# The last steps of a graph layer on one core: two bases a step later, one block's statistics moved, and a quad's second layer ahead of older sums

## The chip, the cores and the metric

The kernel runs on one NeuronCore of one Trainium2 chip. The metric is the device time of one execution in microseconds (us), as the median of several runs. A profiled execution gives the trace. The engines are called as in the profile: PE is TensorE, DVE is VectorE, ACT is ScalarE, POOL is GpSimd and SP is SyncE. "ACTq" and "SPq" are instructions of a queue that only issue transfers.

## What is computed

12500 nodes with 128 features and 400000 edges sorted by destination. Each edge turns its length into 50 radial functions, sends them through two layers to 128 weights, and multiplies those with the projected features of its source node. The products are summed per destination. Each node's sum goes through two more layers, is added to twice the node's features and normalized over the features.

```python
rbf = jnp.exp(-(distances[:, None] - centers) ** 2 / (2.0 * width * width))
cut = 0.5 * (jnp.cos(jnp.pi * distances / CUTOFF) + 1.0) * (distances <= CUTOFF)
W = (jax.nn.silu(rbf @ fw1 + fb1) @ fw2 + fb2) * cut[:, None]
messages = (h[src] @ pw + pb) * W
agg = jax.ops.segment_sum(messages, dst, num_segments=num_atoms)
h_new = h + (jax.nn.silu(agg @ mw1 + mb1) @ mw2 + mb2)
...
y = x + h_new
out = (y - mean(y)) / sqrt(var(y) + eps)        # over the features
```

## The kernel before

The order of all instructions is written out by hand: an engine runs its instructions in the order in which the program issues them, and waits at the first one whose data aren't there.

**Quads.** Edges that are too long to count are left out first; the others are handled in quads of 512 edges, 4 columns of 128. There are 139 quads, 0 to 138 (`NL = 139`). The main loop over `q` and, behind it, steps written out one by one handle quad after quad. The last seven, 132 to 138, are these written steps (the first is `q = NL - 7`). "Step 134" below is what the program issues for quad 134. One step uses:

- `fetch` (L1088): POOL gathers the source rows, one indirect transfer for each column, three or four for a quad, many quads ahead of their use. Quads 133 and 134 have their first column brought row by row by SP and ACT, long before.
- `basis(o)` (L1140, L1144): ACT makes the radial functions of two quads, `2o` and `2o+1`, with a square and an exponential. The exponential needs a table load (ACT_TABLE_LOAD, on ACT) where another function ran before; so do the silu and the square root of other steps.
- `first(o)` (L1156, PE) and `silu(o)` (L1162, ACT): the first layer of the same two quads. Of the last two bases, 68 serves quads 136 and 137, and 69 serves quad 138.
- `second(q)` (L1171 with L1174, PE): the second layer of one quad, into one of four banks of PSUM. Step q calls it for quad q+2.
- `message(q)` (L1189, for row-by-row columns L1186, DVE): the second layer's output times the gathered rows. It frees the bank. The last quad's message is made in four slices, one for each column.
- `place(q)` (L1201, DVE): the one-hot matrices of the destinations, with the cutoff in them.
- `sum_up(q)` (L1221, PE): message times one-hot matrix, into `sums`.
- `add(q)` (L1255, DVE): `sums` is added to the table `aggT`, at two positions.

**Node blocks.** As soon as the destinations of a block of nodes are complete, its nodes are finished in between: `node_first` (L1267 with L1268 on PE, silu L1270 on ACT into `zs`, both through a bank), `node_second` (L347 with L350, PE, into a bank), `node_stats` (L1305 and L1309, DVE: sum with the features, mean and variance), `deviations` (small DVE operations and a square root on ACT, L1325), `scales` (L1335, L1336), `normalize` (L1356 on ACT, or L1353 on DVE) and a transfer to the output (L193, SP or ACT). Blocks are named by their first tile of 128 nodes: 64, 68, 72 and 76 are the last that the loop handles by a computed table (`begin`), 80 and 84 have four tiles, and 88, 90, 92, 94 and 96 have two. `node_x` (L1285, L1288) adds the features of block 96 on PE, and `node_rest` (L1295) its second layer. `load_x` and `store` bring features in and results out.

**Banks.** `second`, `node_first`, `node_second` and `node_x` each take the bank that has been free longest, so that one of them can wait until an engine has emptied that bank.

`keep_busy(n)` (L1439 before, L1442 in the change) runs n matrix multiplications whose result nobody uses.

## Time and profile before

| | |
|---|---|
| median of 3 runs | 720.64 us (720.64 to 723.32) |
| the profiled execution's own time | 718.53 us |
| its span, first to last instruction | 717.0 us |
| busy over the span: PE, DVE, ACT, POOL | 82%, 78%, 56%, 74% |
| mean granted TensorE clock | 0.918 |

The change reaches only the last tenth of the span. The busy time in that part, in stretches of 5 us (clock as a share of full speed):

| stretch (us) | PE | DVE | ACT | POOL | clock |
|---|---|---|---|---|---|
| 675 to 680 | 2.38 | 3.91 | 4.60 | 3.78 | 1.00 |
| 680 to 685 | 5.00 | 2.53 | 2.25 | 3.78 | 1.00 |
| 685 to 690 | 4.34 | 4.05 | 3.58 | 3.78 | 1.00 |
| 690 to 695 | 3.67 | 3.30 | 3.85 | 3.78 | 1.00 |
| 695 to 700 | 2.61 | 3.84 | 1.79 | 3.78 | 0.90 |
| 700 to 705 | 5.00 | 2.72 | 1.43 | 1.06 | 0.76 |
| 705 to 710 | 3.81 | 3.48 | 4.54 | 0.00 | 1.00 |

A row of a timeline below gives the start in us, the busy time in us, engine, line, operation, output and inputs with shapes and count; in brackets stands how long the engine had been idle before it, and what ended that. A row of the chain of waits gives start, length and what the end of the program waited for in that time.

### The profile page before, as it was taken

How to read it: one execution, taken by the hardware profiler on the slowest of the kernel's cores; microseconds unless marked ns; L12 is line 12 of the kernel's file. 1: busy time of each engine (PE TensorE's matmuls, PEld its weight loads, DVE VectorE, ACT ScalarE, POOL GpSimd, SP SyncE). 2: the span in 40 equal slices, each digit the busy share in tenths (PEclk: the TensorE clock that was granted, in tenths of full speed). 3: DMA queues.
4: the chain of work that ended last, by engine and by line, in shares of the span. 5: the costliest groups of instructions: out<-in, count | busy, mean ns of one | idle time of the engine just before them, and what ended most of it. 6: DMA issues, size and time to landing. Idle time of an engine off the chain costs nothing.

```text
span 717.0 us, 14503 instructions
## 1 busy us (share of the span) xinstructions
PE 584.6 (82%) x3526; PEld 461.1 (64%) x3526; DVE 561.7 (78%) x1741; ACT 401.7 (56%) x569; POOL 529.2 (74%) x565
## 2 busy tenths in 40 slices
PE   5878868688898788697878997799998887878775
PEld 5767557566676576575666765577686654665554
DVE  8899899759998799989979994876856545555765
ACT  6557625245645667554645566466765843574564
POOL 6777777777777777777777777777777777777771
PEclk9998787899999899889987999699999998999997
DMA  8996533333334333443344334444543444344242
GB/s 259 328 328 206 161 99 102 98 102 84 115 103 130 83 87 100 118 126 85 87 113 118 99 116 116 130 131 120 153 113 91 138 111 114 101 142 126 56 131 79
DMA packets 54004, 91.41 MB, mean 127 GB/s; under 512 B 14272, under 2 KB 21536, under 8 KB 53914
## 3 DMA queue, kind: packets, MB, share of 16 engines
q0 software_dynamic: 17712, 36.51, 20.4%
q1 hardware_dynamic: 24916, 35.61, 15.0%
q10 hardware_dynamic: 11286, 18.31, 8.0%
q8 instruction: 29, 0.48, 0.3%
q14 instruction: 61, 0.50, 0.2%
HBM read 74.59 MB, written 15.79 MB: 126 GB/s over the span
## 4 chain that ended last, share of the span: by engine, by line
POOL 18%; DVE 15%; DMA 13%; issue 13%; PE 9%; ACT 3%; ACTq 3%; DVEq 1%; SPq 0%; POOLq 0%
POOL quad L1088 14%; DMA quad<-proj,srci 8%; POOL x L1088 3%; DVE hot L1201 3%; PE ph L1156 3%; DMA x<-proj,srci 3%; DVE msg L1189 2%; ACTq L1064 2%; PE sums L1221 2%; PE bank L1174 1%; DVE aggT L1255 1%; DMA packed<-line,at_i 1%; DVE quad L1189 1%; DMA pair<-packed 1%; DVE quad L1201 1%
## 5 line engine op out<-in xcount | busy, mean ns | idle before, releaser
L1088 POOL DMA_INDIRECT quad<-proj,srci x402 | 381.7, 950 | 122.6 <-issue 97.3
L1174 PEld LDWEIGHTS bank<-fw_sb,s 128*128 128x128 f32 x1112 | 158.1, 205 | 60.3 <-issue 50.2
L1174 PE MATMUL bank<-fw_sb,s 128*128 128x128 f32 x1112 | 158.2, 289 | 0.0
L1156 PE MATMUL ph<-rbf,w_sb 102*128 102x512 f32 x278 | 143.7, 642 | 12.3 <-ACT s L1162 8.3
L1221 PEld LDWEIGHTS sums<-hot,msg 128*128 128x128 f32 x816 | 109.2, 200 | 53.4 <-issue 26.0
L1162 ACT ACTIVATE s<-ph 128x1024 f32<-128x1024 f32 x70 | 71.2, 1017 | 122.3 <-PE ph L1156 121.9
L1201 DVE TENSOR_SCALAR hot<-iota_n,dl,cut 128x80 f32<-128x80 f32 (+4 forms) x408 | 111.1, 347 | 22.9 <-PE sums L1221 20.9
L1221 PE MATMUL sums<-hot,msg 128*128 128x80 f32 (+4 forms) x816 | 111.5, 282 | 15.4 <-DVE msg L1189 15.2
L1088 POOL DMA_INDIRECT x<-proj,srci x94 | 90.0, 958 | 28.7 <-issue 22.3
L1171 PE MATMUL bank<-fb_b,ones_b 96*128 96x512 bf16 x139 | 56.0, 403 | 42.2 <-DVE msg L1189 22.0
L1189 DVE TENSOR_TENSOR msg<-bank,quad 128x512 f32<-128x512 f32 (+1 forms) x78 | 52.5, 673 | 41.1 <-DMA quad<-proj,srci 34.5
L1156 PEld LDWEIGHTS ph<-rbf,w_sb 102*128 102x128 f32 x278 | 51.2, 205 | 51.7 <-issue 37.3
L1255 DVE TENSOR_TENSOR aggT<-aggT,sums 128x80 f32 (+4 forms) x209 | 54.1, 259 | 30.7 <-PE sums L1221 12.4
L1140 ACT ACTIVATE rbf<-d_sb,rbf_bias,rbf_scale 102x512 f32<-102x512 f32 x70 | 56.2, 803 | 8.0 <-issue 8.0
L1088 POOL DMA_INDIRECT quad<-in_x_dram,srci x48 | 47.5, 990 | 15.9 <-issue 12.5
L1162 ACT ACT_TABLE_LOAD x34 | 43.6, 1283 | 15.3 <-issue 14.9
L1144 ACT ACT_TABLE_LOAD x35 | 44.9, 1283 | 11.4 <-issue 9.6
L1221 PE MATMUL sums<-quad,quad 128*128 128x128 f32 (+3 forms) x296 | 41.8, 285 | 11.0 <-DVE quad L1189 11.0
L350 PEld LDWEIGHTS bank<-pw_sb,xT 128*128 128x128 f32 (+1 forms) x292 | 42.3, 209 | 11.2 <-issue 5.6
L1144 ACT ACTIVATE rbf<-rbf 102x512 f32<-102x512 f32 x70 | 44.1, 630 | 7.9 <-issue 5.6
L1221 PEld LDWEIGHTS sums<-quad,quad 128*128 128x128 f32 x296 | 38.6, 201 | 12.7 <-DVE quad L1189 12.4
L350 PE MATMUL bank<-pw_sb,xT 128*128 128x128 f32 (+1 forms) x292 | 42.8, 293 | 0.8 <-ACT xT L995 0.6
(281 smaller groups left out, 796.9 us busy)
## 6 DMA issues: line engine op xcount, KB each, us to landing
d_sb<-near_d ACTq DMA_DIRECT2D x67, 256.0 KB
row_sb<-proj SPq DMA_DIRECT2D x1024, 0.5 KB
x<-in_x_dram SPq DMA_DIRECT2D x46, 256.0 KB
row_sb<-proj ACTq DMA_DIRECT2D x512, 0.5 KB
quad<-proj,srci POOLq DMA_INDIRECT x402
proj<-hp SPq DMA_DIRECT2D x24, 256.0 KB
out_dram<-x SPq DMA_DIRECT2D x22, 256.0 KB
x<-proj,srci POOLq DMA_INDIRECT x94
```

The costliest lines, as they stand in the source:

```text
L350: nc.tensor.matmul(to[:m, k, :], lT[:, k * P:k * P + m], w, start=False, stop=(k == a + c - 1))
L1088: g = nc.gpsimd.indirect_dma_start(out=got[:, j, :], out_offset=None, in_=proj if table is None else table, in_offset=bass.IndirectOffsetO ...
L1140: a = nc.scalar.activation(rbf[:u], d[:u], AF.Square, bias=rbf_bias[:u], scale=rbf_scale[:u])
L1144: nc.scalar.activation(rbf[:u], rbf[:u], AF.Exp, scale=-1.0 / (2.0 * width * width))
L1156: nc.tensor.matmul(ph[:, h, :], w1_sb[:2 * KR, h, :], rbf[:2 * KR], start=True, stop=True)
L1162: nc.scalar.activation(s[:, :n], ph[:, :n], AF.Silu)
L1171: nc.tensor.matmul(pu, ones_b[:, :P], bias_b["fb2"].rearrange("k j f -> k (j f)"), start=True, stop=False)
L1174: nc.tensor.matmul(pu[:, j * H:(j + 1) * H], s[:, j * P:(j + 1) * P], fw2_sb, start=False, stop=(j == QT - 1))
L1189: nc.vector.tensor_mul(msg[:, a:b, :], pu_of[q].rearrange("p (j f) -> p j f", j=QT)[:, a:b, :], got_of[q][:, a:b, :])
L1201: nc.vector.tensor_scalar(hot[:, j, :wide(q)], iota_n[:, :wide(q)], dl[:, at[0], at[1]], cut[:, at[0], at[1]], op0=OP.is_equal, op1=OP.mult)
L1221: nc.tensor.matmul(pa[:, k * W:k * W + wide(q)], msg[:, j, :], hot[:, j, :wide(q)], start=(j % n == 0), stop=(j % n == n - 1))
L1255: nc.vector.tensor_add(to, to, pa[:, k * W:k * W + wide(q)])
```

## The change

No work of the computation is added or left out. Only the order changes, with five more `keep_busy` multiplications and one more pair of table loads.

- **Bases.** The loop no longer calls `basis` for the last two bases in its last step (131). The written step 132 calls them at its end, behind its node work. Their `first` and `silu` follow in steps 133 and 134.
- **Statistics.** The deviations of blocks 64, 68 and 72 are taken without block 76, at the statistics of 72 (step 129). Block 76 joins 80, 84, 88 and 90, whose deviations are taken in step 135. Its own statistics stand at the end of step 130.
- **Second layer.** In each written step, `second(q + 2)` now stands between the message and `sum_up(q)`; before, it stood behind `sum_up(q)`. In the same way `node_second` of 90 and 92, and `node_x`, come ahead of sums, and `first` in steps 133 and 134.
- **The end.** Normalizing of 76 and 80 stands together in step 136, block 88 is normalized on DVE, and `keep_busy` is called with 3, 2 and 2 in place of 1 and 1.

```diff
@@ nodes
-            if begin[t0][2] == q:
+            if begin[t0][2] == q and t0 != early[-1]:
                 if k % 4 == 0:
                     st_of[0] = statistics()
                 node_stats(t0, st_of[0][:, k % 4 * 4:])
-                if k % 4 == 3:
+                if k % 4 == 3 or t0 == early[-2]:
                     deep.append(deviations(early[k // 4 * 4:k + 1], st_of[0]))
@@ tail
+        if q == NL - 9:
+            last_st.append(statistics())
+            node_stats(early[-1], last_st[0])
@@ main loop
-                if 2 * o < NL:
+                if 2 * o < NL and q < NL - 8:
                     basis(o)
@@ written steps
 q = NL - 7
 house(q)
-sum_up(q, message(q))
+msg = message(q)
 second(q + 2)
+sum_up(q, msg)
+node_second(84)
+node_stats(80, last_st[:, 4:])
 bases_of(list(range(q, NL)))
 place(q + 1)
-scales(*deep.pop(0))
+for o in (octs(q), octs(q + 1)):
+    basis(o)
 add(q)
-first(octs(q))
-silu(octs(q))
-node_second(84)
 normal(1)
-st = statistics()
-node_stats(80, st)
 
 q += 1
 house(q)
-sum_up(q, message(q))
+msg = message(q)
 second(q + 2)
-first(octs(q))
-silu(octs(q))
-normal(1)
+first(octs(q - 1))
+silu(octs(q - 1))
+sum_up(q, msg)
 place(q + 1)
+node_stats(84, last_st[:, 8:])
 add(q)
 node_first(88)
...
 q += 1
 house(q)
-sum_up(q, message(q))
+msg = message(q)
 second(q + 2)
+node_x(96)
+sum_up(q, msg)
 place(q + 1)
-node_x(96)
 st = statistics()
+scales(*dev)
 add(q)
 node_first(92)
-scales(*dev)
-normal(1)
+normal(2)
 place(q + 2)
 
 p, q = NL - 2, NL - 1
 house(p)
-sum_up(p, message(p))
+msg = message(p)
 node_second(92)
+keep_busy(3)
+sum_up(p, msg)
+node_stats(92, st)
 sum_up(q, message(q, (0, 1)), (0,))
 add(p)
 node_first(94)
+sum_up(q, message(q, (1, 2)), (1,))
 normal(1)
-sum_up(q, message(q, (1, 2)), (1,))
-node_stats(92, st)
 add(q, (0,))
+keep_busy(2)
 sum_up(q, message(q, (2, 3)), (2,))
-normal(2)
+normalize(*ready.pop(0), on=(0, 1))
+store()
+normal(1)
 node_second(94)
-keep_busy(1)
 sum_up(q, message(q, (3, 4)), (3,))
 add(q, (1,))
 node_first(96)
 node_stats(94, st[:, 2:])
+keep_busy(2)
 dev = variances([92, 94], st)
-keep_busy(1)
```

How it moves instructions at three places. First ACT, from the silu of block 80 on (`zs_10699`, and `zs_10724` in the change) to the silu of basis 68 (`s_10814`, and `s_10853` in the change); `rbf` are the last two bases, and `x41` to `x44` are blocks 64 to 76. Before:

```order
L1270 ACTIVATE zs_10699<-bank3_170 128x512
L1325 ACT_TABLE_LOAD
L1325 ACTIVATE dev_10714<-v_10709,eps_121 128x16
L1140 ACTIVATE rbf_10724<-d_sb,rbf_bias_155,rbf_scale_154 102x512
L1144 ACT_TABLE_LOAD
L1144 ACTIVATE rbf_10724<-rbf_10724 102x512
L1140 ACTIVATE rbf_10728<-d_sb,rbf_bias_155,rbf_scale_154 102x512
L1144 ACTIVATE rbf_10728<-rbf_10728 102x512
L1270 ACT_TABLE_LOAD
L1270 ACTIVATE zs_10755<-bank1_168 128x512
L1162 ACTIVATE s_10814<-ph_10811 128x1024
```

Now:

```order
L1270 ACTIVATE zs_10724<-bank3_170 128x512
L1356 ACTIVATE x42_88<-x42_88,by_10671,rs_10670 128x128 x4
L1270 ACTIVATE zs_10762<-bank2_169 128x512
L1140 ACTIVATE rbf_10822<-d_sb,rbf_bias_155,rbf_scale_154 102x512
L1144 ACT_TABLE_LOAD
L1144 ACTIVATE rbf_10822<-rbf_10822 102x512
L1140 ACTIVATE rbf_10826<-d_sb,rbf_bias_155,rbf_scale_154 102x512
L1144 ACTIVATE rbf_10826<-rbf_10826 102x512
L1356 ACTIVATE x43_89<-x43_89,by_10671,rs_10670 128x128 x4
L1162 ACT_TABLE_LOAD
L1162 ACTIVATE s_10853<-ph_10850 128x1024
```

The silu of block 84 (`zs_10755`, now `zs_10762`) has come from behind the square root, both bases and a table load to ahead of them; block 72 is normalized between the bases and the silu of basis 68.

Second PE, steps 132 and 133. `hot0` is the one-hot matrix of quad 132 and `hot1` that of 133; `ph` is the first layer of basis 68; the two rows L347 and L350 are `node_second(84)`. Before, from the sums of 132 on:

```order
L1221 MATMUL sums_10762<-hot0_1075,msg0_1080 128x128 x4
L1171 LDWEIGHTS ones_b_130
L1171 MATMUL bank1_168<-fb2_b_133,ones_b_130 128x512
L1174 MATMUL bank1_168<-fw2_sb_118,s_10642 128x128 x4
L1156 MATMUL ph_10811<-rbf_10724,w1_sb_114 128x512 x2
L347 LDWEIGHTS ones_b_130
L347 MATMUL bank0_167<-mb2_b_135,ones_b_130 128x512
L350 MATMUL bank0_167<-mw2_sb_120,zs_10755 128x128 x4
L1221 MATMUL sums_10762<-hot1_1192,msg1_680 128x128 x4
```

Now, from the second layer of 134 on:

```order
L1171 MATMUL bank2_169<-fb2_b_133,ones_b_130 128x512
L1174 MATMUL bank2_169<-fw2_sb_118,s_10651 128x128 x4
L1221 MATMUL sums_10774<-hot0_1075,msg0_1080 128x128 x4
L347 LDWEIGHTS ones_b_130
L347 MATMUL bank0_167<-mb2_b_135,ones_b_130 128x512
L350 MATMUL bank0_167<-mw2_sb_120,zs_10762 128x128 x4
L1171 LDWEIGHTS ones_b_130
L1171 MATMUL bank3_170<-fb2_b_133,ones_b_130 128x512
L1174 MATMUL bank3_170<-fw2_sb_118,s_10651 128x128 x4
L1156 MATMUL ph_10850<-rbf_10822,w1_sb_114 128x512 x2
L1221 MATMUL sums_10774<-hot1_1192,msg1_680 128x128 x4
```

The second layer of 134 has moved ahead of the sums of 132, and that of 135 ahead of the sums of 133; the first layer of basis 68 now stands right ahead of the sums of 133, and `node_second(84)` two items earlier.

Third PE in step 136 (`hot0` is quad 136, `hot1` quad 137; L1285 and L1288 are `node_x(96)`, L1267 and L1268 `node_first(92)`). Before:

```order
L1221 MATMUL sums_10971<-hot0_1075,msg0_1080 128x128 x4
L1171 LDWEIGHTS ones_b_130
L1171 MATMUL bank2_169<-fb2_b_133,ones_b_130 128x512
L1174 MATMUL bank2_169<-fw2_sb_118,s_10851 128x128 x4
L1285 LDWEIGHTS ones_b_130
L1285 MATMUL bank0_167<-mb2_b_135,ones_b_130 128x256
L1288 MATMUL bank0_167<-x43_89,ident_68 128x128 x2
L1288 MATMUL bank0_167<-x43_89,ident_68 84x128 x2
L1267 LDWEIGHTS mb1_b_134
L1267 MATMUL bank3_170<-ones_b_130,mb1_b_134 128x256
L1268 MATMUL bank3_170<-aggT_99,mw1_sb_119 128x256
L1221 MATMUL sums_10971<-hot1_1192,msg1_680 128x128 x4
```

Now:

```order
L1171 MATMUL bank3_170<-fb2_b_133,ones_b_130 128x512
L1174 MATMUL bank3_170<-fw2_sb_118,s_10889 128x128 x4
L1285 LDWEIGHTS ones_b_130
L1285 MATMUL bank1_168<-mb2_b_135,ones_b_130 128x256
L1288 MATMUL bank1_168<-x43_89,ident_68 128x128 x2
L1288 MATMUL bank1_168<-x43_89,ident_68 84x128 x2
L1221 MATMUL sums_10976<-hot0_1075,msg0_1080 128x128 x4
L1267 LDWEIGHTS mb1_b_134
L1267 MATMUL bank0_167<-ones_b_130,mb1_b_134 128x256
L1268 MATMUL bank0_167<-aggT_99,mw1_sb_119 128x256
```

The second layer of 138 and `node_x(96)` have moved from behind the sums of 136 to ahead of them.

More of the change, by code (lines that the diff above doesn't have):

```diff
@@ L1425, in nodes @@
                 load_x(t0)
-    st_of, deep = {}, []
+    st_of, deep, last_st = {}, [], []
     def tail(q):
+        if q == NL - 9:
+            last_st.append(statistics())
+            node_stats(early[-1], last_st[0])
         for k, t0, step in ((9, 80, node_first), (8, 80, node_second), (8, 84, node_first)):
@@ L1645, in normal @@
             store()
-    assert not todo and counted and not ready and len(deep) == 1 and done[0] == NL - 7
+    assert not todo and counted and not ready[1:] and not deep and done[0] == NL - 7
+    last_st = last_st[0]
     q = NL - 7
     house(q)
-    sum_up(q, message(q))
+    msg = message(q)
     second(q + 2)
+    sum_up(q, msg)
+    node_second(84)
+    node_stats(80, last_st[:, 4:])
     bases_of(list(range(q, NL)))
     place(q + 1)
-    scales(*deep.pop(0))
+    for o in (octs(q), octs(q + 1)):
+        basis(o)
     add(q)
-    first(octs(q))
-    silu(octs(q))
-    node_second(84)
     normal(1)
-    st = statistics()
-    node_stats(80, st)
     q += 1
     house(q)
-    sum_up(q, message(q))
+    msg = message(q)
     second(q + 2)
-    first(octs(q))
-    silu(octs(q))
-    normal(1)
+    first(octs(q - 1))
+    silu(octs(q - 1))
+    sum_up(q, msg)
     place(q + 1)
+    node_stats(84, last_st[:, 8:])
     add(q)
     node_first(88)
-    node_stats(84, st[:, 4:])
     load_x(92)
@@ L1677 @@
     house(q)
-    sum_up(q, message(q))
+    msg = message(q)
     second(q + 2)
+    first(octs(q - 1))
+    silu(octs(q - 1))
+    sum_up(q, msg)
     node_second(88)
@@ L1682 @@
     add(q)
-    normal(1)
     node_first(90)
-    node_stats(88, st[:, 8:])
+    node_stats(88, last_st[:, 12:])
     load_x(94)
-    normal(1)
     q += 1
     house(q)
-    sum_up(q, message(q))
+    msg = message(q)
     second(q + 2)
     node_second(90)
+    sum_up(q, msg)
     place(q + 1)
+    node_stats(90, last_st[:, 14:])
+    dev = deviations([76, 80, 84, 88, 90], last_st)
+    silu_next()
     add(q)
     load_x(96)
-    node_stats(90, st[:, 10:])
-    dev = deviations([80, 84, 88, 90], st)
-    silu_next()
     q += 1
     house(q)
-    sum_up(q, message(q))
+    msg = message(q)
     second(q + 2)
+    node_x(96)
+    sum_up(q, msg)
     place(q + 1)
-    node_x(96)
     st = statistics()
+    scales(*dev)
     add(q)
     node_first(92)
-    scales(*dev)
-    normal(1)
+    normal(2)
     place(q + 2)
```

## Prediction

> **What bounds the kernel now.** I read the chain of waits first, then POOL's timeline, then DVE's, and asked for each of the last quads how long its message waited, or was late. The chain ends its long stretch of gathers at quad 131:

> ```profile
> 644.16 2.45 DMA quad<-proj,srci
> ...
> 652.90 4.10 DMA quad<-proj,srci
> ...
> 667.90 2.50 DMA quad<-proj,srci
> ```

> A gather lands 2.5 us after its start (4.1 once). POOL starts them 1.25 us apart, with 0.30 us of idle time each, up to the last one. These are the last gathers of quads 131, 134, 135, 136 and 137, and all four of 138:

> ```profile
> 667.90 0.94 POOL L1088 DMA_INDIRECT quad<-proj,srci  x1 [0.30 <-issue]
> ...
> 680.44 0.94 POOL L1088 DMA_INDIRECT quad<-proj,srci  x1 [0.30 <-issue]
> ...
> 685.44 0.94 POOL L1088 DMA_INDIRECT quad<-proj,srci  x1 [0.30 <-issue]
> ...
> 690.43 0.94 POOL L1088 DMA_INDIRECT quad<-proj,srci  x1 [0.30 <-issue]
> ...
> 695.44 0.94 POOL L1088 DMA_INDIRECT quad<-proj,srci  x1 [0.30 <-issue]
> 696.68 0.94 POOL L1088 DMA_INDIRECT quad<-proj,srci  x1 [0.30 <-DVE st L1309]
> 697.93 0.94 POOL L1088 DMA_INDIRECT quad<-proj,srci  x1 [0.30 <-issue]
> 699.18 0.94 POOL L1088 DMA_INDIRECT quad<-proj,srci  x1 [0.30 <-issue]
> 700.42 0.94 POOL L1088 DMA_INDIRECT quad<-proj,srci  x1 [0.30 <-issue]
> ```

> The messages of 131, 134, 135, 136, 137 and the last two slices of 138:

> ```profile
> 670.53 0.69 DVE L1189 TENSOR_TENSOR quad<-bank,quad 128x512 f32<-128x512 f32 x1 [0.85 <-DMA quad<-proj,srci]
> ...
> 686.97 0.55 DVE L1189 TENSOR_TENSOR quad<-bank,quad 128x384 f32<-128x384 f32 x1
> ...
> 692.12 0.69 DVE L1189 TENSOR_TENSOR quad<-bank,quad 128x512 f32<-128x512 f32 x1
> ...
> 697.34 0.69 DVE L1189 TENSOR_TENSOR msg<-bank,quad 128x512 f32<-128x512 f32 x1
> ...
> 701.37 0.68 DVE L1189 TENSOR_TENSOR msg<-bank,quad 128x512 f32<-128x512 f32 x1
> ...
> 706.29 0.48 DVE L1189 TENSOR_TENSOR quad<-bank,quad 128x128 f32<-128x128 f32 x2
> ```

> Start plus 2.5 us against start of the message: quad 131 lands at 670.4 and starts at 670.5. Then 134 is 4.0 us late (682.9 against 687.0), 135 4.2, 136 4.4, 137 3.4, and the last slice of 138, which lands at 702.9 and starts at about 706.5, is 3.6 late. So up to 131 the gathers bound the kernel, and behind it the order of the other engines does. The 3.6 us are what an order can win ahead of the last slice; POOL itself stays, since the change leaves its instructions alone.

> Where the lateness arises is seen on ACT and PE:

> ```profile
> 675.34 1.12 PE L1268 MATMUL bank<-aggT,mw_sb 128*128 128x512 f32 x2 [0.30 <-DVE aggT L1255]
> ...
> 679.72 0.38 PE L1171 MATMUL bank<-fb_b,ones_b 96*128 96x512 bf16 x1 [2.32 <-ACT zs L1270]
> ...
> 683.66 1.06 PE L1221 MATMUL sums<-hot,msg 128*128 128x128 f32 x8
> 684.55 0.38 PE L1171 MATMUL bank<-fb_b,ones_b 96*128 96x512 bf16 x1
> 684.77 1.05 PE L1174 MATMUL bank<-fw_sb,s 128*128 128x128 f32 x8
> 685.66 1.02 PE L1156 MATMUL ph<-rbf,w_sb 102*128 102x512 f32 x2
> 686.52 0.27 PE L1267 MATMUL bank<-ones_b,mb_b 96*128 96x256 bf16 x1
> 686.64 0.59 PE L1268 MATMUL bank<-aggT,mw_sb 128*128 128x256 f32 x2
> 687.11 1.40 PE L1221 MATMUL sums<-quad,quad 128*128 128x128 f32 x8
> ```

> ```profile
> 673.65 0.80 ACT L1140 ACTIVATE rbf<-d_sb,rbf_bias,rbf_scale 102x512 f32<-102x512 f32 x1
> ...
> 677.78 1.28 ACT L1270 ACT_TABLE_LOAD   x1
> 679.07 0.60 ACT L1270 ACTIVATE zs<-bank 128x512 f32<-128x512 f32 x1
> ```

> Block 84's first layer is through PE at 676.46, but its silu runs at 679.07, behind both bases (673.65 to 677.78) and a table load. PE needs that bank and stands 2.32 us; the sums of 133 come at 683.66, and DVE's add, node work and message of 134 behind them.

> **Part by part.**

> *Bases and statistics of 76.* With the bases behind it, block 84's silu can follow its first layer. The wait of 2.32 us goes; the sums of 133, 3.94 us behind its end (679.72 to 683.66), are no longer behind `node_second(84)` either. The price is one more square root and silu table, 1.28 us each, in step 129, where ACT waits for block 72's statistics anyway. That silu of block 76 comes some 5 us later; PE asks for it in step 130, so at most some tenths are lost, and step 131 to 132 has more than that in hand.

> The bases themselves now lie on the path to step 134. ACT takes 4.1 us for both (673.65 to 677.78). From about 675.7 that ends at 679.8; block 72's normalizing (four tiles, 1.6) and the silu table (1.3) follow, and basis 68's silu ends near 683.5. PE wants it for the second layer of 136 at about 684.3. It fits by 0.8 us.

> *Second layer ahead of sums.* By the starts above, a second layer takes 1.11 us (684.55 to 685.66), half a first layer 0.86, `node_first` of two tiles 0.59, sums 0.89. Counted on PE from one quad's sums to the end of the next: laying these durations out in the new order, basis 68's first layer (two halves) begins near 680.0, behind the second layer of 135, and the sums of 133 end near 682.6. Step 134 has 0.59 + 1.11 + 0.86 + 0.89 = 3.45 and about 1.3 of waiting for the add of 133, so its sums end near 687.3, and message 135 starts near 688.8, 0.9 late. Step 136 has the second layer of 138 (1.11), `node_x` (about 1.0) and sums (0.89), 3.0 in all, against a pace of 5.0 (685.44 to 690.43). The second layer and `node_x` are then done while the message waits for its gather. So message 136 should find its gather just landed, and 137 waits by about 1.3. What stands behind the moved second layer on PE is the sums of its own step, and behind these DVE's add; while PE isn't late for silu, this costs nothing.

> *The last quad.* Message slice at landing instead of 3.6 us later: minus 3.6. After it, before:

> ```profile
> 707.07 0.61 PE L350 MATMUL bank<-mw_sb,zs 128*128 128x128 f32 x4
> 707.51 0.38 PE L1439 MATMUL ph<-mb_b,ones_b 96*128 96x512 bf16 x1
> 707.73 0.38 PE L1221 MATMUL sums<-quad,quad 128*128 128x128 f32 x2
> ...
> 708.49 0.62 PE L1268 MATMUL bank<-aggT,mw_sb 128*128 128x212 f32 x2 [0.29 <-DVE aggT L1255]
> 708.96 0.38 PE L1439 MATMUL ph<-mb_b,ones_b 96*128 96x512 bf16 x1
> 709.66 0.67 PE L1295 MATMUL bank<-mw_sb,zs 128*84 128x128 f32 x4 [0.32 <-ACT zs L1270]
> ```

> The last sums start 1.2 us behind the slice (706.5 to 707.73), since `node_second(94)` and a `keep_busy` came between. With slices 1.25 us apart these fit ahead of the last one: 0.3, so minus 0.9. From the sums on the chain is the same.

> *`keep_busy`.* Five more, 0.22 us each on PE (707.51 to 707.73). Three stand ahead of the sums of 137, where PE waits for a gather; two ahead of the third slice, likewise; of the last two, one is new and fits into the 0.32 us ahead of L1295. Nothing; without cover, 0.7 us for the three.

> *Stores.* Blocks 76 and 80 are now stored at about 698 to 702, while the last gathers are under way. The last gather can then land between 2.45 and 4.10 us after its start instead of 2.5: 0 to plus 1.6. I take plus 0.5, nearer to the many than to the single one.

> *Clock.*

> ```profile
> 699.40:702.50 3.10, 3.10 (x17) 2.95 (x15) 2.74 (x10) 0.00 (x0) 1.66 (x2) 0.52 0.26 63
> ```

> At half clock from 699.2 to 702.5 PE lost 1.7 us, after idling for 2.39 us:

> ```profile
> 698.09 1.31 PE L1221 MATMUL sums<-hot,msg 128*128 128x128 f32 x8 [2.39 <-DVE msg L1189]
> ```

> This is within the 3.6 us, not beside it. [...]

> *Sum:* −3.6 − 0.9 + 0.5 = −4.0 us. The profiled execution took 718.53 us with this span:

> ```profile
> span 717.0 us, 14503 instructions
> ```

> So the span should become 713.0 and its time 714.5. The median of the runs, 720.64, is 2.1 above the profiled one; I take the 4.0 off it: **716.6 us**. Bounds: −4.5 (no collision) and −2.9 (a landing of 4.1), 716.1 to 717.7.

> **The rivals.**

> 1. *The stores meet the last gathers.* Last landing at 4.1 us: −2.9, 717.7. For it, the 4.10 above; against it, every other row near 2.5. 0.15.
> 2. *The clock falls again, nearer the end.* PE still idles by 0.5 to 1 us between slices, and one such stretch costs 1.7: −2.3, 718.3. Against it, the five multiplications. 0.12.
> 3. *The lateness only moves.* If basis 68's silu misses its 0.8 us, PE stands at the second layer of 136 with the sums of 134 behind it, as it did at 679.72, and the backlog of some 3.6 stays. Only the 0.9 is won: 719.7. 0.09.
> 4. *Slower: PE becomes the bound at half clock.* Steps 134 to 137 need some 3.5 us of PE each; at half clock 7.0 to 7.2, 2.2 more than the pace of 5.0. Over 684 to 701, 3.5 steps, this is 7.5 late and 3.5 worse than before: 724.1. It decides once half clock lasts over 9 us (4.0 by 2.2 per 5.0). Against it: the stretch shown lasted 3.3. 0.09.

> **How the numbers follow.** Forecast 0.55, rivals 0.15, 0.12, 0.09, 0.09. What a measurement can tell here is about 0.5%, 3.6 us, so faster means below 717.0. Of the forecast's 0.55, 0.45 lies there, with 0.05 from rivals 1 and 2: faster 0.50. The rest of these and rival 3 make the same: 0.41. Rival 4: slower 0.09. The range reaches from 714.9, 1.2 below the forecast's own for terms mis-sized, to 720.0, which takes in rivals 1 to 3.

> **What would show it.** Right: block 84's silu directly behind its first layer, no wait near 2.3 us at L1171 in step 132; messages 136 to 138 with DVE idle ahead of them, ended by a gather; last slice at 703 to 703.5; clock 1.00 from 690 on. POOL's last gather still starts at 700.4. Wrong: L1171 or L1174 waiting for silu in step 134, the last slice beyond 705, a last gather above 3.5 us, or POOL waiting for a buffer.

## The result, and the profile after

| | before | changed |
|---|---|---|
| median (us) | 721.40 (720.64 to 723.32) | 717.32 (716.44 to 718.55) |
| ratio, with its 95% interval | 1 | 0.9944 (0.9928 to 0.9960) |
| the profiled execution's own time | 718.53 | 718.55 |
| its span | 717.0 | 717.0 |
| last gather's start to the end of the span | 16.6 | 15.0 |

The change makes the kernel faster by 0.56%, 4.08 us between the medians. The two profiled executions, however, have the same span. That of before was faster than every run of before in this comparison (2.9 us below their median), that of the change the slowest of its six (1.2 us above its median). And POOL's last gather starts at 700.42 in the one and at 701.99 in the other. The difference is there long before the change reaches anything: the gather that stands 40 ahead of the last starts at 650.41 and at 651.90. So positions are read below against the gathers of their own execution, and the last row of the table, from the last gather's start to the end, leaves out what happened earlier.

The start of the backlog, PE and then ACT of the changed kernel. Columns as in the timelines before.

```profile
676.18 1.02 PE L1268 MATMUL bank<-aggT,mw_sb 128*128 128x512 f32 x2
677.88 0.38 PE L1171 MATMUL bank<-fb_b,ones_b 96*128 96x512 bf16 x1 [0.68 <-ACT zs L1270]
...
683.82 1.06 PE L1221 MATMUL sums<-hot,msg 128*128 128x128 f32 x8
...
686.21 0.38 PE L1171 MATMUL bank<-fb_b,ones_b 96*128 96x512 bf16 x1
```

```profile
677.24 0.60 ACT L1270 ACTIVATE zs<-bank 128x512 f32<-128x512 f32 x1 [2.27 <-PE bank L1268]
677.73 0.80 ACT L1140 ACTIVATE rbf<-d_sb,rbf_bias,rbf_scale 102x512 f32<-102x512 f32 x1
...
684.69 1.02 ACT L1162 ACTIVATE s<-ph 128x1024 f32<-128x1024 f32 x1
686.41 0.38 ACT L1270 ACTIVATE zs<-bank 128x256 f32<-128x256 f32 x1 [0.69 <-PE bank L1268]
```

Block 84's silu now starts 1.06 us behind the start of the matmul that it waits for (3.73 before), the bases stand behind it, and PE's wait is 0.68 us where it was 2.32.

The messages of 134 to 137 and the last slice, on DVE:

```profile
685.73 0.55 DVE L1189 TENSOR_TENSOR quad<-bank,quad 128x384 f32<-128x384 f32 x1
690.92 0.69 DVE L1189 TENSOR_TENSOR quad<-bank,quad 128x512 f32<-128x512 f32 x1
695.03 0.68 DVE L1189 TENSOR_TENSOR msg<-bank,quad 128x512 f32<-128x512 f32 x1
699.62 0.69 DVE L1189 TENSOR_TENSOR msg<-bank,quad 128x512 f32<-128x512 f32 x1 [0.80 <-DMA quad<-proj,srci]
...
706.59 0.29 DVE L1189 TENSOR_TENSOR quad<-bank,quad 128x128 f32<-128x128 f32 x1 [2.41 <-DMA quad<-proj,srci]
```

Against these, the last gathers of 135, 136, 137 and 138 on POOL:

```profile
687.01 0.94 POOL L1088 DMA_INDIRECT quad<-proj,srci  x1 [0.30 <-DMA quad<-proj,srci]
...
692.00 0.94 POOL L1088 DMA_INDIRECT quad<-proj,srci  x1 [0.30 <-issue]
...
697.00 0.94 POOL L1088 DMA_INDIRECT quad<-proj,srci  x1 [0.30 <-issue]
...
701.99 0.94 POOL L1088 DMA_INDIRECT quad<-proj,srci  x1 [0.30 <-DMA quad<-proj,srci]
```

"Late" is counted as in the prediction, from the landing of a quad's last gather to the start of its message. With 2.42 us for a landing (next view), message 135 is 1.5 us late instead of 4.2, 136 0.6 instead of 4.4, and 137 waits 0.80 us for its gather. So the backlog is small from the start and gone at 137. But the last slice, too, waits for its gather, and that one is late by itself. The chain of waits:

```profile
699.49 2.42 DMA quad<-proj,srci
...
701.99 4.58 DMA quad<-proj,srci
...
706.59 0.30 DVE quad L1189
...
709.07 0.85 PE ph L1442 x2
709.92 0.79 PE bank L1295 x4
```

4.58 us instead of 2.42. PE's timeline there:

```profile
706.93 0.69 PE L1221 MATMUL sums<-quad,quad 128*128 128x128 f32 x2 [2.17 <-DVE quad L1189]
...
708.00 1.07 PE L1268 MATMUL bank<-aggT,mw_sb 128*128 128x212 f32 x2 [0.20 <-DVE aggT L1255]
```

PE was idle for 2.17 us before the last sums, and then the clock was at half speed. The stretches of 2 us, in the columns of the earlier windows (PE, PEld, DVE, ACT, POOL, then clock, DMA share, GB/s):

```profile
706.00:708.00 2.00, 0.87 (x4) 0.43 (x4) 0.64 (x3) 0.00 (x0) 0.00 (x0) 0.77 0.66 226
708.00:710.00 2.00, 2.00 (x6) 1.23 (x7) 1.41 (x8) 0.81 (x2) 0.00 (x0) 0.50 0.00 0
```

At that clock the two multiplications of `keep_busy` (L1442) stand on the chain with 0.85 us, and L1268 takes 1.07 where it took 0.62. From the last slice's start to the end of the span it takes 10.4 us; before, from 706.5, it was 10.5. The 0.9 us expected there were not won in this execution.

### The profile page after: what moved, and what is told of

The parts are those of the page before. It is cut to its first block, busy times and chain, and to the rows that moved or that the text cites. A ratio compares the mean times of both kernels' runs of the same rounds, so it can differ in the third digit from the quotient of the medians.

```text
span 717.0 us, 14516 instructions
## 1 busy us (share of the span) xinstructions
PE 591.3 (82%) x3531; PEld 466.5 (65%) x3531; DVE 562.5 (78%) x1743; ACT 402.2 (56%) x568; POOL 529.0 (74%) x565
## 5 line engine op out<-in xcount | busy, mean ns | idle before, releaser
L1088 POOL DMA_INDIRECT quad<-proj,srci x402 | 382.0, 950 | 125.0 <-issue 91.5
L1174 PEld LDWEIGHTS bank<-fw_sb,s 128*128 128x128 f32 x1112 | 160.6, 208 | 55.1 <-issue 44.8
L1174 PE MATMUL bank<-fw_sb,s 128*128 128x128 f32 x1112 | 160.8, 292 | 0.0
L1156 PE MATMUL ph<-rbf,w_sb 102*128 102x512 f32 x278 | 144.9, 646 | 11.8 <-ACT s L1162 7.7
L1221 PEld LDWEIGHTS sums<-hot,msg 128*128 128x128 f32 x816 | 111.1, 203 | 49.2 <-issue 26.1
L1221 PE MATMUL sums<-hot,msg 128*128 128x80 f32 (+4 forms) x816 | 113.0, 284 | 11.5 <-DVE msg L1189 11.3
L1088 POOL DMA_INDIRECT x<-proj,srci x94 | 89.6, 953 | 28.7 <-issue 21.0
L1171 PE MATMUL bank<-fb_b,ones_b 96*128 96x512 bf16 x139 | 56.4, 406 | 37.3 <-DVE msg L1189 21.2
L1189 DVE TENSOR_TENSOR msg<-bank,quad 128x512 f32<-128x512 f32 (+1 forms) x78 | 52.5, 673 | 42.9 <-DMA quad<-proj,srci 42.1
L1156 PEld LDWEIGHTS ph<-rbf,w_sb 102*128 102x128 f32 x278 | 51.9, 208 | 52.2 <-issue 38.5
L1255 DVE TENSOR_TENSOR aggT<-aggT,sums 128x80 f32 (+4 forms) x209 | 54.0, 258 | 27.3 <-PE bank L1268 9.0
L1140 ACT ACTIVATE rbf<-d_sb,rbf_bias,rbf_scale 102x512 f32<-102x512 f32 x70 | 56.2, 803 | 7.9 <-issue 7.9
L1088 POOL DMA_INDIRECT quad<-in_x_dram,srci x48 | 47.2, 983 | 15.4 <-issue 12.5
L1221 PE MATMUL sums<-quad,quad 128*128 128x128 f32 (+3 forms) x296 | 42.4, 288 | 10.3 <-DVE quad L1189 10.1
L350 PEld LDWEIGHTS bank<-pw_sb,xT 128*128 128x128 f32 (+1 forms) x292 | 42.5, 211 | 12.7 <-issue 6.9
L1221 PEld LDWEIGHTS sums<-quad,quad 128*128 128x128 f32 x296 | 39.0, 203 | 12.3 <-DVE quad L1189 11.5
L350 PE MATMUL bank<-pw_sb,xT 128*128 128x128 f32 (+1 forms) x292 | 43.8, 298 | 0.8 <-ACT xT L995 0.6
```

The source lines that it names most:

```text
L350: nc.tensor.matmul(to[:m, k, :], lT[:, k * P:k * P + m], w, start=False, stop=(k == a + c - 1))
L1088: g = nc.gpsimd.indirect_dma_start(out=got[:, j, :], out_offset=None, in_=proj if table is None else table, in_offset=bass.IndirectOffsetO ...
L1140: a = nc.scalar.activation(rbf[:u], d[:u], AF.Square, bias=rbf_bias[:u], scale=rbf_scale[:u])
L1156: nc.tensor.matmul(ph[:, h, :], w1_sb[:2 * KR, h, :], rbf[:2 * KR], start=True, stop=True)
L1171: nc.tensor.matmul(pu, ones_b[:, :P], bias_b["fb2"].rearrange("k j f -> k (j f)"), start=True, stop=False)
L1174: nc.tensor.matmul(pu[:, j * H:(j + 1) * H], s[:, j * P:(j + 1) * P], fw2_sb, start=False, stop=(j == QT - 1))
```

## The experiments

**Theory:** the new order removes a backlog that begins at block 84's silu. **Rivals:** one of its parts does it alone, or the added multiplications and the clock do it. About the end, the first theory was that the stores of 76 and 80 hold up the last gather; the rival, that one gather landed late by chance.

Times are compared with runs of the kernel before on the same chip. Two groups of runs fell on a chip on which every kernel, the one before included, took 1052 to 1083 us; they are told last and bear on no conclusion.

| | median (us) | ratio to before (95%) | last gather's start to end (us) | last landing (us) |
|---|---|---|---|---|
| before | 720.0 to 721.4 | 1 | 16.6 | 2.20 |
| the whole change | 717.32 | 0.9944 (0.9928 to 0.9960) | 15.0 | 4.09 |
| bases alone | 718.29 | 0.9971 (0.9959 to 0.9982) | 16.4 | 2.19 |
| second layers alone | 720.85 | 1.0018 (1.0004 to 1.0033) | 18.8 | 2.24 |
| change, stores held | 715.98 | 0.9941 (0.9924 to 0.9958) | 13.6 | 3.20 |
| change, fetch earlier | 715.75 | 0.9945 (0.9925 to 0.9966) | 12.7 | 2.37 |
| change, both | 715.78 | 0.9937 (0.9922 to 0.9952) | 12.6 | 2.17 |

The last two columns are of each kernel's one profiled execution. The landing there is counted from the gather's start on POOL to the end of its last packet; it is shorter than in the chain of waits, which counts until DVE's wait ends (4.09 against 4.58 in the changed kernel). One execution need not be typical of its kernel: for the bases alone it was the slowest of twelve.

### The bases alone

```diff
-                if 2 * o < NL:
+                if 2 * o < NL and q < NL - 8:
                     basis(o)
@@ step 132
     scales(*deep.pop(0))
+    for o in (octs(q), octs(q + 1)):
+        basis(o)
     add(q)
-    first(octs(q))
-    silu(octs(q))
@@ steps 133 and 134, behind second(q + 2)
+    first(octs(q - 1))
+    silu(octs(q - 1))
```

> Before, with one part alone: the last two bases a step later. Theory: the wait of 2.32 us in step 132 goes, but the second layer still stands behind the sums, so part of the lateness of the messages stays: minus 1.5 to minus 3 us, 0.996 to 0.998. Rival A (the place of the bases is all): 0.9944 as the whole change. Rival B (the added multiplications and the clock are all): 1.000. PE's fetch falls where it did before, behind the last sums.

Measured: 0.9971 (0.9959 to 0.9982), 1.9 us between the medians, 718.29 against 720.15. The theory's interval holds, and both rivals are out: it is neither the whole nor nothing. In the profile the wait in step 132 is gone, as the first PE row below shows, which has no idle time in front of it. But another stall stands two steps later. Timelines of ACT, PE and DVE:

```profile
688.34 1.02 ACT L1162 ACTIVATE s<-ph 128x1024 f32<-128x1024 f32 x1 [1.29 <-PE ph L1156]
689.26 1.63 ACT L1356 ACTIVATE x<-x,by,rs 128x128 f32<-128x128 f32 x4
690.79 0.36 ACT L1270 ACTIVATE zs<-bank 128x256 f32<-128x256 f32 x1
```

```profile
680.29 0.38 PE L1171 MATMUL bank<-fb_b,ones_b 96*128 96x512 bf16 x1
...
688.25 0.60 PE L1268 MATMUL bank<-aggT,mw_sb 128*128 128x256 f32 x2
...
691.21 0.38 PE L1171 MATMUL bank<-fb_b,ones_b 96*128 96x512 bf16 x1 [1.47 <-ACT zs L1270]
```

```profile
693.93 0.42 DVE L1305 SCALAR_TENSOR_TENSOR x<-x,bank 128x256 f32<-128x256 f32 x1 [3.55 <-PE bank L350]
...
694.97 0.69 DVE L1189 TENSOR_TENSOR quad<-bank,quad 128x512 f32<-128x512 f32 x1
...
700.18 0.69 DVE L1189 TENSOR_TENSOR msg<-bank,quad 128x512 f32<-128x512 f32 x1
...
704.01 0.68 DVE L1189 TENSOR_TENSOR msg<-bank,quad 128x512 f32<-128x512 f32 x1
```

Block 88's first layer is through PE at 688.85. Its silu stands behind basis 68's silu (688.34) and the normalizing of one older block (1.63 us), PE waits 1.47 us for the bank, DVE 3.55 us for block 88's second layer, and message 135, in DVE's order behind that, starts at 694.97. In the changed kernel (ACT above) no normalizing stands between 684.69 and block 88's silu at 686.41: with the deviations of 76 taken later, there is none to do in that step.

So in this trace the backlog isn't smaller. Messages 135, 136 and 137 are 4.1, 4.3 and 3.1 us late (their last gathers start at 688.46, 693.45 and 698.45), against 4.2, 4.4 and 3.4 before, and from the last gather to the end it takes 16.4 us against 16.6. The 1.9 us lie between the medians, and where they arise this trace doesn't show.

### The second layers alone

```diff
@@ steps 132 to 136
-    sum_up(q, message(q))
+    msg = message(q)
     second(q + 2)
+    sum_up(q, msg)
```

> Before, with one part alone: the second layer of a later quad between the message and the sums in the written steps. The bases alone gave 0.9971, about half of the whole change. Theory (the stall behind the bases decides, and this part only pays once it is gone): PE still waits some 2.3 us in step 132, now ahead of the sums, and from the last gather's start to the end of the span it takes 16 to 17 us as before (16.6): 0.999 to 1.001. Rival A (each part gives its half by itself): 14 to 15 us, 0.997. Rival B (the sums stand behind the stall as well, and the adds come later): 17 us or more, 1.0015 or above.

Measured: 1.0018 (1.0004 to 1.0033), and 18.8 us from the last gather to the end. Rival A is out. Rival B fits best, but the lower end of the interval lies within the theory's range as well. PE's timeline and a stretch of the windows:

```profile
675.82 1.12 PE L1268 MATMUL bank<-aggT,mw_sb 128*128 128x512 f32 x2 [0.79 <-DVE aggT L1255]
680.20 0.58 PE L1171 MATMUL bank<-fb_b,ones_b 96*128 96x512 bf16 x1 [3.26 <-ACT zs L1270]
```

```profile
680.00:685.00 5.00, 4.80 (x19) 4.19 (x19) 0.73 (x4) 0.15 (x1) 3.78 (x5) 0.50 0.22 56
```

The second layer waits for the same bank as before, but now the sums of 132 wait with it: 3.26 us instead of 2.32, with half clock behind that. The parts don't add up: minus 1.9 and plus 0.9 us are far from the minus 4.1 of the whole. That the second layers pay once the stall is gone is likely, but not shown, since the whole change also has the statistics and the added multiplications, and no run outside the other chip (last part of this section) has the bases and the second layers together without the statistics.

### The stores held back

Every store behind the last message slice gets a wait for that slice; blocks 76 to 90 are normalized where the change has them.

```diff
-    normal(2)
+    normalize(*ready.pop(0))
+    normalize(*ready.pop(0))
...
-    store()
-    normal(1)
+    normalize(*ready.pop(0))
     node_second(94)
     sum_up(q, message(q, (3, 4)), (3,))
+    store()
```

> The change, but the stores of blocks 76, 80, 84, 88 and 90 wait until the last quad's last message slice is made, so that no store meets a gather; everything else as changed. Theory (the stores hold the last gather up): every one of the last four gathers lands 2.2 to 2.7 us after its start, the last slice is made within 0.3 us of that, PE has no wait near 2 us ahead of the last sums, and the time falls by 1 to 2.5 us on the changed kernel: 714.8 to 716.3 us, 0.990 to 0.993 of before. Rival (the landing of 4.58 us was one odd gather): the time of the changed kernel, 0.9944 within 0.0015. Rival (the held stores come too late and end the kernel): the span ends with stores that land behind block 92's, 0.996 or above.

Measured: 715.98 us lies where the theory had it, but it is 0.9941 of a before that was also lower, so the ratio is that of the changed kernel. And the last gather still lands late, in 3.88 us:

```profile
700.26 3.88 DMA quad<-proj,srci
704.16 0.30 DVE quad L1194
```

So it isn't the stores alone, and two executions of two speak against chance. The DMA queues in the stretch in which the last gather is under way (q0 carries the gathers, q1 what SP issues), in this kernel, 701 to 704.2 us, and in the changed one, 702 to 706:

```profile
q0 software_dynamic: 41, 0.07, 7.8%
q8 instruction: 1, 0.02, 2.7%
```

```profile
q1 hardware_dynamic: 211, 0.37, 25.2%
q0 software_dynamic: 63, 0.13, 12.9%
q8 instruction: 1, 0.02, 2.5%
```

Before, from 700 to 704 us:

```profile
q0 software_dynamic: 71, 0.13, 13.0%
```

One packet of 16 KB on a queue for instructions (q8) is what both have and before has not. The packets of that time in the trace, start to end in us:

```
stores held    q8 16384 B  701.66 to 703.02
               q0  4096 B  15 packets 701.91 to 702.38, the 16th 703.01 to 703.45
changed        q8 16384 B  703.25 to 704.88
               q1  2048 B  on from 704.86, three of them of 0.21 to 0.23 us
               q0  4096 B  15 packets 703.93 to 704.40, the 16th 705.91 to 706.07
before         q0  4096 B  16 packets 702.08 to 702.61
               q8 16384 B  707.66 to 709.03
```

A gather is 16 packets of 4 KB. The page of the profile counts 16 DMA engines, so this is taken to be one packet for each; the trace doesn't say on which engine a packet ran. With the stores held, the sixteenth starts (703.01) when the fetch of instructions ends (703.02), as if it had stood behind it; in the changed kernel another microsecond passes (704.88 to 705.91), in which packets of a store run. That it waited for the fetch is inferred from these times, and the next two runs test it. These fetches are taken to be PE's, by their places: in the traces of before and of the changed kernel each comes 99 to 143 matmuls behind the one before (the very last excepted), and the last but one comes when 3513 matmuls have started, in the changed kernel as with the stores held, and at 3516 before. With five more multiplications and a PE that is less late, that place in the program is passed while the last gather is under way; before, it was passed 7 us later.

### The fetch moved forward, with and without the stores held

Forty more multiplications without use ahead of it bring the fetch to an earlier step.

```diff
         if q % 4 < 2 and 2 * octs(q) < NL:
+            if q >= NL - 47:
+                keep_busy(2)
             first(octs(q))
             silu(octs(q))
```

> The change, with 40 more multiplications without use on PE, two ahead of each of the twenty first layers in steps 92 to 129; nothing else is altered, and the stores go out as changed. New theory: PE's instructions are fetched in blocks of 16 KB by one transfer of 1 to 1.6 us on one of the DMA engines; in the changed kernel the last such fetch but one starts 1.3 us behind the start of the very last gather, whose packet on that engine has to wait. 40 more multiplications ahead of it bring the same fetch forward to 694 to 697 us, where the gathers have time to spare: the last gather lands at most 3.3 us after its start (the stores can still meet it), against 4.6, and the time is 0.5 to 2 us below the changed kernel, 0.9915 to 0.9937 of before. Rival (the landing depends on the stores alone, or is chance): it stays near 4 us or scatters, 0.9944 within 0.0015. Rival (the 40 multiplications make PE late, or the fetch hurts as much where it now falls): 0.996 or above.

> The same with 40 more multiplications, and with the stores of blocks 76 to 90 held until the last message slice is made. If the fetch and the stores were both in the way of the last gather: all of the last four gathers land 2.2 to 2.6 us after their starts, the last slice comes 9.7 us ahead of the span's end at full clock, and the time is 1.5 to 3 us below the changed kernel, 0.990 to 0.9925 of before. If only the stores or only chance delayed it: no better than with held stores alone, 0.9941 within 0.0015.

Measured: the fetch comes at 692.7 and at 693.9 us, when 3500 and 3499 matmuls have started: nearly the same count as without the forty (3513), reached some 9 us earlier against the last gather. The last gather, started at 700.40 and at 701.64, lands in 2.37 us beside the stores and in 2.17 without them (4.09 and 3.20 with the fetch on it). The last slices, DVE:

```profile
703.15 0.29 DVE L1189 TENSOR_TENSOR quad<-bank,quad 128x128 f32<-128x128 f32 x1
```

```profile
704.13 0.29 DVE L1194 TENSOR_TENSOR quad<-bank,quad 128x128 f32<-128x128 f32 x1
```

In neither does the clock fall before PE's last matmul (1.00 in every stretch from 690 to 708 us), and from the last gather to the end it takes 12.7 and 12.6 us instead of 15.0. That the fetch held the last gather up is shown by this: it was moved, and the delay went with it, with the stores still there. In the seven profiles of the table, the last gather lands late in the two in which a fetch falls on it (3.20 and 4.09 us) and in 2.17 to 2.37 us in the other five. In these single executions the stores alone cost 0.2 us (2.37 against 2.17), and 0.9 where they come on top of the fetch (4.09 against 3.20).

The times don't follow as expected. 0.9945 and 0.9937 lie within the interval of the changed kernel, and only the second is a little below it in the middle. 2.3 us would be 0.32%. The profiled execution of the changed kernel was itself 1.2 us above its median (718.55 against 717.32), so that half of the 2.3 us may belong to that execution alone; the other half, 0.16%, is less than these intervals can tell. So neither version is shown to beat the changed kernel, and how much the late landing costs in an average execution is open.

### Runs on the other chip

> The changed kernel once more, as the yardstick of this group. Theory (the order wins, the stores meet the last gather): 716.4 to 718.5 us, 0.993 to 0.996 of before. Chance or not: the profiled execution of the changed kernel had a last gather that landed 4.58 us after its start, with the store of block 80 issued 0.07 us behind that start. If the stores do it, this profile has again a last gather above 3.3 us; if it was one odd landing, it shows 2.2 to 2.6.

> The change without its part on statistics: block 76 keeps its place among 64, 68 and 72, its statistics in step 131, and its normalizing and its store in the old steps; bases, second layers and multiplications as changed. Theory (this part only makes room on ACT, and costs by its stores beside the last gathers): the last gather lands 2.2 to 2.6 us after its start, and the time is the changed kernel's or up to 1.5 us below, 0.9915 to 0.995. Rival (the square root and the statistics of 76 in step 131 hold up the silu of block 84): basis 68 comes 1 to 2 us later, the second layer of 136 waits, plus 1 to plus 2 on the changed kernel, 0.996 to 0.998.

> The changed kernel again, as yardstick and to see whether the late landing recurs. Theory (PE's fetch of 16 KB falls on the last gather, at the same place of PE's program in every execution, and the stores of 76 and 80 lie beside it): a fetch starts 1.0 to 1.8 us behind the start of the last gather, which lands 3.2 to 4.7 us after its start; from the last gather's start to the end of the span 13.5 to 15 us, where the two kernels with the earlier fetch had 12.7 and 12.6; 0.9944 of before within 0.0015. Rival (it was one odd execution): 2.2 to 2.6 us, and 12.6 to 13 us to the end.

> The change without its part on the statistics: block 76 stays among 64, 68 and 72, and is normalized and stored in the old steps; only the store of block 80 is left beside the last gathers. Theory (this part is worth nothing by itself; PE's program is as long as in the changed kernel, so the fetch still meets the last gather): 0.9944 within 0.0015, the last gather lands 3.0 to 4.0 us after its start. Rival A (the square root of 76 in step 131 holds up the silu of block 84 and the bases): the second layer of 136 waits for basis 68's silu, 1 to 2 us above the changed kernel, 0.996 to 0.9975. Rival B (the two stores were the whole cost at the end): 0.992 to 0.993.

The change without its part on statistics was, against the changed kernel:

```diff
-            if begin[t0][2] == q and t0 != early[-1]:
+            if begin[t0][2] == q:
...
-    dev = deviations([76, 80, 84, 88, 90], last_st)
+    dev = deviations([80, 84, 88, 90], last_st)
...
+    scales(*deep.pop(0))
     for o in (octs(q), octs(q + 1)):
         basis(o)
```

| kernel | ratio to before (95%) | second time |
|---|---|---|
| the change again | 0.9898 (0.9845 to 0.9950) | 1.0017 (0.9973 to 1.0060) |
| bases alone | 0.9961 (0.9930 to 0.9991) | |
| second layers alone | 1.0056 (1.0017 to 1.0095) | 1.0009 (0.9966 to 1.0053) |
| statistics undone | 1.0008 (0.9968 to 1.0047) | 0.9973 (0.9919 to 1.0028) |

The same kernel differs between the two times by more than any effect studied here. The windows of one of them, the bases alone, in a span of 1059.1 us, show why the last steps can't be read there:

```profile
1000.00:1010.00 10.00, 6.95 (x46) 5.69 (x45) 2.44 (x9) 1.62 (x2) 4.75 (x5) 0.98 0.15 40
1010.00:1020.00 10.00, 8.59 (x31) 6.22 (x30) 6.52 (x24) 3.47 (x4) 0.00 (x0) 0.50 0.28 80
```

POOL has started its last gather by 1010, 50 us ahead of the end, so no last step waits for a gather. What slows that chip is not known. So the part on statistics has no measurement of its own, and neither have the added multiplications, whose number wasn't varied in the last steps.

## Why the prediction was right, and where it wasn't

The forecast was 716.6 us within 714.9 to 720.0, most likely faster. Measured were 717.32 us and faster. The start of the backlog was understood rightly; at the end of the kernel the profiled execution went another way than forecast. Step by step:

- **The cause, block 84's silu behind both bases: right, but not enough by itself.** The wait of 2.32 us became 0.68, and the lateness of 135 to 137 went with it. With the bases alone moved, 1.9 us of the 4.1 came between the medians, but the profile of that run shows the wait gone and the lateness still there, behind a new stall.
- **The bases fit by 0.8 us: right.** The second layer of 136 starts at 686.21 without a wait in step 134; the silu that it needs ends at 685.71, 0.5 us earlier.
- **The statistics as a mere price of some tenths: incomplete.** The prediction gave this part no gain. With the bases alone, ACT normalizes an older block ahead of block 88's silu and message 135 starts 4.1 us late (694.97, its last gather started at 688.46); in the changed kernel that normalizing is not there. The second layers by themselves cost 0.9 (720.85 against 719.99), so the remaining 2.2 us come from the statistics, from the second layers once the bases are moved, from the added multiplications, or from these together. That the statistics have a part in it is argued from the two profiles, not measured.
- **Second layers ahead of sums: right only together with the rest.** "While PE isn't late for silu, this costs nothing" was the condition, and alone, with that silu late, the part cost 0.18%. The times forecast behind it were close: message 135 0.9 us late (measured 1.5), 136 at its gather's landing (0.6 late), 137 waiting by about 1.3 (0.80).
- **Last slice at landing, minus 3.6: right in kind.** It waits for the gather, 2.41 us long. At 703.0 to 703.5 it wasn't: 1.6 us are the later gather of that execution, 2.1 the late landing.
- **Stores, plus 0.5: the term that was mis-sized.** In the profiled execution the last landing took 2.1 us more (4.58 against 2.45), beyond the bound of 4.10, and mainly by another mechanism: PE's fetch of instructions (16 KB from 703.25 to 704.88), which the prediction didn't have. For the stores alone the single executions give 0.2 (2.37 against 2.17), and 0.9 on top of the fetch (4.09 against 3.20). "POOL itself stays, since the change leaves its instructions alone" held for the starts and not for the landings.
- **Minus 0.9 behind the slice, and `keep_busy` at nothing: wrong in this execution.** The late landing left PE idle for 2.17 us, half a clock followed, and the two multiplications then stood on the chain with 0.85 us. That is rival 2, and what brought it on is the late landing of rival 1. Without the fetch it came out: 12.6 and 12.7 us from the last gather to the end, and the forecast's span of 713.0 with the gather at 700.42 means 12.6.
- **The clock:** the prediction counted the half clock of before within the 3.6 us and expected 1.00 from 690 on. In the changed kernel the clock halved at 707.1, behind a gap of PE of 2.17 us, the longest there from 660 on. Before, half clock followed a gap of 2.39 us and did not follow one of 2.32 (at 679.72).
- **The signs:** two of those named for a wrong prediction came, the last slice beyond 705 (706.59) and a last gather above 3.5 us (4.58), and the clock wasn't 1.00 from 690 on (0.50 from 707.1). Of those named for a right one came the silu of block 84 and step 132 without a wait near 2.3 us; message 137 and the last slice waited for a gather, 136 didn't.
- **The median, and luck:** the sum of −4.0 was taken off the median, and between the medians lie 4.08. That this agrees so closely is in part luck. The two profiles have equal spans, and from the last gather to the end the changed one gains 1.6 us, not 4.0; the profiled execution of before lay 2.9 us below its median, that of the change 1.2 us above. The terms of the sum can be checked in these executions only. The last slice came 4.6 us behind the last gather's start instead of 6.1, so −3.6 + 0.5 = −3.1 became −1.5, and −0.9 became −0.1.

## What to carry to other kernels

Where an order is written by hand, look for the engine whose queue has long work ahead of a short operation that another engine waits for. Moving it paid here (0.9971 alone), but the next such place came up right behind it, so the parts of such a move have to be tried together as well as one by one. Look also at what is fetched: here the fetch of a block of instructions delayed a gather (3.20 and 4.09 us to land, against 2.17 to 2.37 without it), it came at nearly the same place of the program in the five profiles in which that was counted (3499 to 3516 matmuls started), and when PE came by there decided which transfer it met. Compare late steps against an anchor of the same execution, here the last gather's start, since what comes before can differ by more than the effect (that gather started between 700.26 and 703.50 in the seven profiles).

## What was not expected of the hardware

**Instructions, by their places taken to be PE's, came in blocks of 16 KB** during these runs. The page of the changed kernel lists 29 packets on the queue:

```profile
q8 instruction: 29, 0.48, 0.3%
```

By the packets, one took 0.94 to 1.37 us in the last 70 us of before and 0.96 to 1.63 in those of the changed kernel. With the stores held, the gather that met one took 3.20 us from start to last packet, against 2.18 to 2.21 of the three gathers ahead of it.

**The clock changed on a grid of 3.41 us in these traces.** In the changed kernel, in windows of half a microsecond (PE, PEld, DVE, ACT, POOL, then clock, DMA share, GB/s):

```profile
706.50:707.00 0.50, 0.07 (x1) 0.07 (x1) 0.29 (x1) 0.00 (x0) 0.00 (x0) 1.00 1.03 336
707.00:707.50 0.50, 0.50 (x3) 0.36 (x3) 0.00 (x0) 0.00 (x0) 0.00 (x0) 0.58 0.59 195
...
710.00:710.50 0.50, 0.50 (x4) 0.48 (x2) 0.00 (x0) 0.50 (x1) 0.00 (x0) 0.50 0.00 0
710.50:711.00 0.50, 0.20 (x2) 0.00 (x0) 0.26 (x2) 0.49 (x3) 0.00 (x0) 1.00 0.18 49
```
